# A recurrent block with four heads and a feed-forward part on one Trainium2 core: local attention scores laid out with the keys as rows

## The chip, the core and the metric

The kernel runs on one core of one Trainium2 chip (trn2). A core has TensorE (PE in the profile; its weight loads are PEld), VectorE (DVE), ScalarE (ACT), GpSimd (POOL) and SyncE (SP, which here only issues DMAs). The metric is the device time of one execution in microseconds (us). Everything is float32, and each float32 matmul of the program shows as two passes in the trace.

## The reference

The input is x, 8 sequences of 1024 tokens of 512 numbers. One layer is computed:

```
xn = layernorm(x)
s  = concat(local(xn), sparse(xn), memory(xn), prediction(xn)) @ warboss_w + warboss_b
g  = silu(relu(xn @ w1 + b1) @ w2 + b2)          # 512 -> 2048 -> 512
out = x + s * g

local :  softmax(q k^T / sqrt(128)) v            # all 1024 keys
sparse:  the same with its own weights, but only the 102 largest scores of a row count
memory:  attention over a bank of 64 rows, then a linear layer
prediction: three linear layers with a gelu
```

The change lies in `local`. For each of the 8 sequences it makes a 1024 x 1024 matrix of scores, takes each query's softmax over the keys, and multiplies by v. Its weights are scaled so that the scores are large, so the softmax needs each query's maximum taken off first.

## The kernel before, in words

A sequence b has 8 tiles of 128 tokens (i), 4 pairs of tiles (p, 256 tokens, T) and 2 groups (g, 512 tokens). Tokens are normalized and turned so that features lie on the partitions (`xnT`, `turn_tokens`, L328). All big products (feed-forward up and down, q, k, the memory and prediction inputs, the output projection) are made block-wise with seven products in place of eight, so sums of weight blocks (`form_chunk`), of tokens (`token_sums`, L535), of hidden values (`hidden_sums`, L627: tile `hs`) and of results (`add_products`: tiles `u` and `m`) are made around the matmuls, nearly all of them on POOL.

**The order of the work** is decided while the program is built. `feed_forward` (L662) is a filler that yields one PE matmul after another. Beside it stand `chains`: generators such as `local`, `sparse`, `memory_head`, which give out a few instructions and then yield either a time or a condition. `run` (L133) always lets the first chain that is due go on and otherwise takes the next matmul of the filler. Time is counted in PE columns (`clock`), and each instruction adds a planned cost to its engine's clock: a transpose 64 columns on PE, a 512-column copy 360 on ACT, a POOL operation 60 + 1.42 for each element, a round of the sparse selection 1552 on DVE. `pool_is_free` (L507) is a condition that holds when POOL's clock is at most 300 columns ahead of PE's. `STEP` (L1068) is the number of columns from the start of one tile to the start of the next. On the chip each engine takes its instructions in exactly the order written, and waits where data are not there yet. PSUM has four buffers (`ring`, L190) for everything but the feed-forward sums.

**Sparse.** `sparse` (L885) makes a tile's scores with queries as rows, and DVE finds the 102nd largest of each row in 13 rounds of MAX8 and MATCH_REPLACE8 (`sparse_select`). The result `es` is scaled, transposed in eight 128x128 blocks (`transpose_probs`, L791: tile `ptp`, copied to `pT`) and multiplied with v (`attend`, L804).

**Local before.** `local` (L820) runs for each tile: two score matmuls of 128 queries by 512 keys (`scores`, tile `sc`), copied by ACT to `el`; DVE takes each row's maximum (`nml`); ACT computes Exp with that as bias and adds up the row's total; DVE inverts the total (`r_l`); ACT scales `el` by it; PE transposes eight blocks into `ptp`, and ACT copies them to `pT` (keys as rows, queries as columns). At the second tile of a pair, `attend` multiplies v with `pT` for 256 queries at once: 8 matmuls of 256 columns, and the copy `head`.

**After local**, `finish_pair` (L976) makes the sums `ho` of the four heads on POOL, the filler makes the output projection (`ph_po`), and gating and the residual follow.

**The start.** `first_tokens` (L1043) normalizes and turns the first sequence's tokens group by group, projects the sparse keys of 512 tokens (`project_k`, L342) and the first queries, and starts `turn_constants` (L272, which turns the biases and the memory bank) and the first token sums.

Of the kernel before, what the change touches and what calls it, by code (L numbers as in the profile page):

```python
# [9 lines left out]
F32 = mybir.dt.float32  # L10
AF = mybir.ActivationFunctionType
# [4 lines left out]
P = 128  # L16
# [4 lines left out]
def kernel(  # L21
# [144 lines left out]
    def transpose(out, in_, ident):  # L166
        pe.transpose(out, in_, ident)
        tick(P // 2)
# [21 lines left out]
    def ring(name, shape):  # L190
        return ps_r.tile(list(shape), F32, tag="r", name=name)
# [96 lines left out]
    qT = {}  # L288
# [3 lines left out]
    def needs(*keys):  # L292
        return lambda: all(k in done for k in keys)
# [45 lines left out]
        if b not in kT:  # L339
            kT[b] = sb.tile([P, 2, S], F32, tag="kT", name=f"kT_{b}")  # L340

    def project_k(b, g, h, w):  # L342

        make_k(b)
        ps = ring(f"pk_{b}_{g}_{h}", (P, 512))
        accumulate(
            ps,
            [w[:, c, ts(h, HD)] for c in range(ND)],
            [xnT[b, g][:, c, :] for c in range(ND)],
            512,  # L350
        )
        copy(kT[b][:, h, ts(g, 512)], ps, 360)
        done.add(("k", b, g, h))

    def project_v(b, q, w):

# [178 lines left out]
    def token_sums(g, name):  # L535

        b, q = divmod(g, NG)
        if g:
            yield needs(*[("xnT", b, 4 * q + j) for j in range(4)])
            yield after("act", 0)  # L540
        t = sb.tile([P, 4, 2, T], F32, tag="t", name=f"t_{name}")
        xs = xnT[b, q]
        b11, b12, b21, b22 = (xs[:, ts(h, 2), ts(j, T)] for h in range(2) for j in range(2))
        on_pool("tensor_sub", t[:, 0], b12, b11)
        on_pool("tensor_sub", t[:, 1], b22, t[:, 0])
        on_pool("tensor_sub", t[:, 2], b22, b12)
        on_pool("tensor_sub", t[:, 3], b21, t[:, 1])
        yield after("pool")
        tokens[g] = (b11, b21, t[:, 1], t[:, 2], t[:, 3], t[:, 0], b22)

    SLOTS = ((1, 4), (6, 5))
# [221 lines left out]
    def scores(b, i, h, s):  # L773

        for c in range(S // 512):
            ps = ring(f"sc_{b}_{i}_{h}_{c}", (P, 512))
            matmul(
                ps, qT[b, i // 2][:, h, ts(i % 2, P)], kT[b][:, h, ts(c, 512)], True, True, 512
            )
            copy(s[:, ts(c, 512)], ps, 360)  # L780

    def normalize(e, total, name):
        r = small.tile([P, 1], F32, tag="r", name=f"r_{name}", bufs=4)
        dve.reciprocal(r, total)
# [19 lines left out]
    def attend(b, p, h):  # L804
        ps = ring(f"pa_{b}_{p}_{h}", (P, T))
        accumulate(
            ps,
            [vv[b][:, k, h, :] for k in range(NT)],
            [probsT[b, p, h][:, k, :] for k in range(NT)],
            T,  # L810
        )
        o = sb.tile([P, T], F32, tag=f"head{h}", name=f"head_{b}_{p}_{h}")
        copy(o, ps, 220)
        heads[b, p, h] = o
        done.add(("head", b, p, h))

    def before_pair(b, p):
        return [] if (b, p) == (0, 0) else [("joined", *divmod(b * NP + p - 1, NP))]

    def local(b, i):  # L820
        yield needs(("q", b, i // 2), *[("k", b, g, LOCAL) for g in range(NG)])
        yield after("act", 0)
        if (b, i) != (0, 0):
            yield needs(("pT", *divmod(b * NT + i - 1, NT), LOCAL))
        e = sb.tile([P, S], F32, tag="el", name=f"el_{b}_{i}")
        scores(b, i, LOCAL, e)
        done.add(("local scores", b, i))
        yield after("act")
        nm = small.tile([P, 1], F32, tag="nm", name=f"nml_{b}_{i}", bufs=4)
        dve.tensor_reduce(nm, e, AX.X, ALU.max, negate=True)  # L830
        on("dve", 740)
        yield after("dve", 100)
        total = small.tile([P, 1], F32, tag="total", name=f"totl_{b}_{i}", bufs=4)
        act.activation(e, e, AF.Exp, bias=nm, accum_out=total)
        on("act", 800)
        yield after("act", 100)
        yield from normalize(e, total, f"l_{b}_{i}")
        yield from transpose_probs(b, i, LOCAL, e)
        if i % 2:
            yield needs(("v", b), *before_pair(b, i // 2))  # L840
            yield after("act")
            attend(b, i // 2, LOCAL)
        done.add(("local", b, i))

    def sparse_scores(b, i):
        s = sb.tile([P, S], F32, tag="s", name=f"s_{b}_{i}", bufs=2)
# [38 lines left out]
    def sparse(b, i):  # L885
        n = b * NT + i
        yield needs(("q", b, i // 2), *[("k", b, g, SPARSE) for g in range(NG)])
        if n > 1:
            yield needs(("chosen", n - 2))
        yield max(clock["pe"], clock["act"]) + (SLACK if n else 100)  # L890
        s = sparse_scores(b, i)
        done.add(("sparse scores", n))
        yield after("act")
        o = {}
        rounds.append(sparse_select(b, i, s, o))
        yield lambda: "nm" in o
        if n:
            yield needs(("pT", *divmod(n - 1, NT), SPARSE))
        e = sb.tile([P, S], F32, tag="es", name=f"es_{b}_{i}")
        act.activation(e, s, AF.Exp, bias=o["nm"])  # L900
        on("act", 700)
        o["e"] = e
        yield lambda: "total" in o
        done.add(("chosen", n))
        yield after("dve", 100)
        yield from normalize(e, o["total"], f"s_{b}_{i}")
        yield from transpose_probs(b, i, SPARSE, e)
        if i % 2:
            yield needs(("v", b), *before_pair(b, i // 2))
            yield after("act")  # L910
            attend(b, i // 2, SPARSE)


    def tmp(name):
# [128 lines left out]
    def first_tokens():  # L1043
        def normalize_tokens(j0, j1):
            for j in range(j0, j1):
                ln_stats(0, j, first_x[j])
            ln_rstd(0, j0, j1)
            return [ln_apply(0, j, first_x[j]) for j in range(j0, j1)]

        due = normalize_tokens(0, 2) + normalize_tokens(2, 4)  # L1050
        for at in range(3):
            load_chunk(at)
        for g in range(NG):
            for j in range(4 * g, 4 * g + 4):
                yield due[j]
                turn_tokens(0, j, first_x[j])
            if g == 0:
                due += normalize_tokens(4, 8)
                form_chunk(0)
            yield after("act", 200)  # L1060
            project_k(0, g, SPARSE, first_k)
            if g == 0:
                project_q(0, 0, first_q)
                start(turn_constants())
                start(token_sums(0, 0), rank=0)
                start(hidden_sums(), rank=-1)

    STEP = int(0.995 * (11775 + NWC * (2 * 7 * T + 2 * 7 * H) // 4))  # L1068
    start(first_tokens())
    start(sparse(0, 0))  # L1070
    run(needs(("sparse scores", 0)))
# [7 lines left out]
    for n in range(B * NT):  # L1079
        b, i = divmod(n, NT)  # L1080
        p = i // 2
        now = begin + n * STEP
        run(lambda: clock["pe"] >= now)
        start(local(b, i))
        if i == 0:
            start(project_values(b), now + 1000)
            if b + 1 < B:
                start(prepare_stats(b + 1), now + (2000 if b else STEP))
        if i == 3 and b + 1 < B:
            start(prepare_tokens(b + 1))  # L1090
        if i % 2:
            def two_heads(b=b, p=p):
                yield needs(("m", b, p), *before_pair(b, p))
                yield after("act")
                t = starts.pop((b, p))
                yield from prediction_head(b, p, t[:, 1])
                yield from memory_head(b, p, t[:, 0])
                start(finish_pair(b, p), rank=2)

            start(two_heads(), now + 1500)  # L1100
        if n + 1 < B * NT:
            start(sparse(*divmod(n + 1, NT)), now + int(0.6 * STEP))
# [35 lines left out]
```

## Time and profile before

| what | us |
|---|---|
| median of three runs | 2895.06 |
| the three runs | 2895.06, 2892.13, 2895.14 |
| the profiled execution | 2892.31 |
| its span, first to last instruction | 2890.3 |
| first matmul starts, last matmul ends | 7.8, 2881.8 |

| engine | busy us | share of the span | instructions |
|---|---|---|---|
| PE | 2848.1 | 99% | 13296 |
| DVE | 2376.7 | 82% | 3202 |
| POOL | 2187.9 | 76% | 2908 |
| ACT | 1672.6 | 58% | 3174 |

Busy time is the time in which at least one instruction of the engine was in flight. Matmuls overlap, so the mean duration of one is longer than the step from one to the next. A row of a group reads: line, engine, operation, out<-in by the program's names, shapes, count, then busy us, mean ns of one, and the idle time of the engine just before these instructions with what ended most of it. Nearly all rows show line 85, a helper that records every operation, so tiles are told apart by their names. The DMA engines are busy between 40 and 70% of each slice, and move 186 GB/s.

### The profile page before, as it was taken

How to read it: one execution, taken by the hardware profiler on the slowest of the kernel's cores; microseconds unless marked ns; L12 is line 12 of the kernel's file. 1: busy time of each engine (PE TensorE's matmuls, PEld its weight loads, DVE VectorE, ACT ScalarE, POOL GpSimd, SP SyncE). 2: the span in 40 equal slices, each digit the busy share in tenths (PEclk: the TensorE clock that was granted, in tenths of full speed). 3: DMA queues.
4: the chain of work that ended last, by engine and by line, in shares of the span. 5: the costliest groups of instructions: out<-in, count | busy, mean ns of one | idle time of the engine just before them, and what ended most of it. 6: DMA issues, size and time to landing. Idle time of an engine off the chain costs nothing. (4 is left out here: it accounts for less than half of the span.)

```text
span 2890.3 us, 38499 instructions
## 1 busy us (share of the span) xinstructions
PE 2848.1 (99%) x13296; PEld 2394.5 (83%) x13296; DVE 2376.7 (82%) x3202; ACT 1672.6 (58%) x3174; POOL 2187.9 (76%) x2908
## 2 busy tenths in 40 slices
PE   8989999999999999999999999999999999999998
PEld 6878888888888888888888888888888888887887
DVE  7999979878698785988769897789967989588696
ACT  3546556665566654656546665556655556465564
POOL 4787867868678696786958879587796887867785
PEclk9999999999999999999999999999999999999999
DMA  5665644655455454454545545455455554544545
GB/s 179 215 243 193 209 160 160 223 179 205 148 178 214 175 201 162 172 213 163 206 165 186 206 177 193 164 204 199 156 196 184 186 203 169 197 146 174 200 168 187
DMA packets 132001, 538.89 MB, mean 186 GB/s; under 512 B 13790, under 2 KB 40432, under 8 KB 131808
## 3 DMA queue, kind: packets, MB, share of 16 engines
q1 hardware_dynamic: 126352, 519.23, 50.7%
q0 software_dynamic: 5456, 17.22, 1.6%
q8 instruction: 105, 1.72, 0.2%
q14 instruction: 88, 0.72, 0.1%
HBM read 500.35 MB, written 36.04 MB: 186 GB/s over the span
## 5 line engine op out<-in xcount | busy, mean ns | idle before, releaser
L85 DVE MAX8 top<-left 128x8 f32<-128x1024 f32 x768 | 943.2, 1228 | 26.7
L85 POOL TENSOR_TENSOR u_up<-u_up 128x256 f32<-128x256 f32 (+1 forms) x640 | 620.8, 976 | 318.7 <-ACT u_up L85 293.9
L85 DVE MATCH_REPLACE8 left<-top,left 128x1024 f32<-128x1024 f32 x704 | 850.6, 1208 | 0.0
L85 PE MATMUL f<-w_down,hs 128*128 128x256 f32 x2048 | 539.0, 380 | 2.1 <-POOL w_down L85 1.7
L85 PE MATMUL ph_up<-t,w_up 128*128 128x256 f32 x2048 | 483.3, 379 | 0.1
L85 PEld LDWEIGHTS f<-w_down,hs 128*128 128x128 f32 x2048 | 383.6, 191 | 61.5 <-issue 9.2
L85 PEld LDWEIGHTS ph_up<-t,w_up 128*128 128x128 f32 x2048 | 383.1, 190 | 60.2 <-issue 12.0
L85 PE MATMUL f<-w_down,h 128*128 128x256 f32 x1536 | 421.7, 380 | 3.4 <-ACT h L85 3.4
L85 ACT COPY u_up<-ph_up 128x512 f32<-128x512 f32 (+1 forms) x512 | 265.5, 531 | 237.8 <-PE ph_up L85 237.2
L85 PE MATMUL ph_up<-xnT,w_up 128*128 128x256 f32 x1536 | 383.1, 380 | 1.4 <-ACT u_up L85 0.9
L85 POOL TENSOR_TENSOR hs<-h 128x128 f32<-128x128 f32 x512 | 241.4, 471 | 171.2 <-PE f L85 135.7
L85 PEld LDWEIGHTS f<-w_down,h 128*128 128x128 f32 x1536 | 288.3, 191 | 50.7 <-issue 9.6
L85 PEld LDWEIGHTS ph_up<-xnT,w_up 128*128 128x128 f32 x1536 | 288.0, 190 | 48.8 <-issue 8.8
L85 PE MATMUL sc<-kT,qT 128*128 128x512 f32 x512 | 240.4, 593 | 0.2 <-ACT el L85 0.2
L85 PE MATMUL pa<-pT,v 128*128 128x256 f32 x1024 | 231.6, 379 | 0.0
L85 ACT ACTIVATE h<-u_up,biasT 128x256 f32<-128x256 f32 x512 | 220.2, 501 | 14.1 <-POOL u_up L85 14.1
L85 DVE TENSOR_REDUCE nml<-el 128x1 f32<-128x1024 f32 x64 | 77.3, 1208 | 181.0 <-ACT el L85 180.8
L85 PEld LDWEIGHTS pa<-pT,v 128*128 128x128 f32 x1024 | 194.4, 190 | 28.1 <-issue 1.0
L85 DVE MAX8 top<-s 128x8 f32<-128x1024 f32 x64 | 78.2, 1223 | 167.7 <-ACT s L85 167.5
L85 ACT COPY pT<-ptp 128x512 f32<-128x512 f32 x256 | 149.5, 588 | 113.7 <-PE ptp L85 113.1
L85 ACT ACT_TABLE_LOAD x139 | 178.3, 1283 | 5.0 <-DVE nms L85 2.0
L85 POOL TENSOR_TENSOR u_po<-u_po 128x256 f32<-128x256 f32 (+1 forms) x155 | 146.4, 951 | 19.8 <-ACT u_po L85 13.4
(151 smaller groups left out, 4574.7 us busy)
## 6 DMA issues: line engine op xcount, KB each, us to landing
w_down<-w_down_dram SPq DMA_DIRECT2D x248, 896.0 KB, 4.7
w_up<-w_up_dram SPq DMA_DIRECT2D x120, 896.0 KB, 4.6
w_po<-w_po_dram SPq DMA_DIRECT2D x62, 896.0 KB, 4.6
xl<-in_L_attn_x_dram SPq DMA_DIRECT2D x64, 256.0 KB, 4.8
xr<-in_L_attn_x_dram SPq DMA_DIRECT2D x64, 256.0 KB, 5.0
out_dram<-xr POOLq DMA_DIRECT2D x62, 256.0 KB, 3.0
xs<-in_L_attn_x_dram SPq DMA_DIRECT2D x56, 256.0 KB, 4.9
w_q<-w_q_dram SPq DMA_DIRECT2D x15, 896.0 KB, 4.6
```

The lines of the kernel that those rows point to most:

```text
L85: r = made(*args, **kwargs)
```

## The change

The scores of `local` are made for a pair of tiles at once with the keys as rows: each of eight key blocks of 128 is the stationary side, the 256 queries are the moving side (tile `sl`). ACT's copies of them go straight into the tile that `attend` reads (`pT`), so these probabilities are not transposed.

- The maximum over keys now lies across partitions and blocks. DVE first reduces the eight blocks, `e.rearrange("p c t -> p t c")`, 2048 elements to 256, read with a stride of 1 KB. `across` then turns the two 128x128 halves on PE (`pma`), DVE reduces them from PSUM to two columns, ACT spreads these over 128 columns each, PE turns them back (`pmb`), and ACT copies: every partition then holds minus the maximum of each query.
- POOL adds that to the scores (four adds of 512), and ACT computes Exp (two of 1024) without bias or total.
- The total is made in the same way: DVE reduces the blocks (for the first four pairs POOL adds them up), and `across` (`pta`, `ptb`) gives its reciprocal on every partition. It is applied after `attend`, as one POOL product on `head`.
- `local` is started for pairs and not for tiles, and it waits for the head of the pair before.
- At the start, the sparse keys are projected for 256 tokens at a time, the constants are turned behind the first pair of tiles, the first token sums are made on DVE instead of POOL, and the first formed chunk of weights comes later.
- `STEP` becomes 25855 columns; it was 25980.

The diff's core:

```diff
-    def project_k(b, g, h, w):
+    def project_k(b, g, h, w, part=0, parts=1):
...
-        copy(kT[b][:, h, ts(g, 512)], ps, 360)
-        done.add(("k", b, g, h))
+        copy(kT[b][:, h, ts(parts * g + part, n)], ps, 360 // parts)
+        if part == parts - 1:
+            done.add(("k", b, g, h))
...
+        on = on_pool if g else on_dve
+        on("tensor_sub", t[:, 0], b12, b11)
...
+    def across(ps_name, part, work, op, negate, name):
+        pt = ring(f"{ps_name}a_{name}", (P, 2, P))
+        for j in range(2):
+            transpose(pt[:, j], part[:, ts(j, P)], ident)
+        of = small.tile([P, 2], F32, tag="of", name=f"of{ps_name}_{name}")
+        dve.tensor_reduce(of, pt, AX.X, op, negate=negate)
+        if not negate:
+            dve.reciprocal(of, of)
+        on("dve", 330)
+        yield after("dve", 200)
+        act.copy(work[:, 2].rearrange("p (j t) -> p j t", j=2), of.unsqueeze(2).to_broadcast([P, 2, P]))
+        on("act", 220)
+        yield after("act", 200)
+        pt = ring(f"{ps_name}b_{name}", (P, 2, P))
+        for j in range(2):
+            transpose(pt[:, j], work[:, 2, ts(j, P)], ident)
+        copy(work[:, 3], pt.rearrange("p j t -> p (j t)"), 220)
...
+    def local(b, p):
...
+        for c in range(0, NT, 2):
+            ps = ring(f"sl_{name}_{c}", (P, 2, T))
+            for u in range(2):
+                matmul(
+                    ps[:, u], kT[b][:, LOCAL, ts(c + u, P)], qT[b, p][:, LOCAL], True, True, T
+                )
+            copy(e[:, c : c + 2], ps, 360)
...
+        dve.tensor_reduce(work[:, 0], e.rearrange("p c t -> p t c"), AX.X, ALU.max)
+        on("dve", 1400)
+        yield after("dve", 200)
+        yield from across("pm", work[:, 0], work, ALU.max, True, name)
+        yield after("act", 200)
+        for c in range(0, NT, 2):
+            yield pool_is_free
+            on_pool(
+                "tensor_add", e[:, c : c + 2], e[:, c : c + 2],
+                work[:, 3].unsqueeze(1).to_broadcast([P, 2, T]),
+            )
+        yield after("pool", 100)
+        for c in range(0, NT, 4):
+            act.activation(e[:, c : c + 4], e[:, c : c + 4], AF.Exp)
+            on("act", 800 - 100 * (c > 0))
+        yield after("act", 100)
+        if n < EARLY:
+            yield pool_is_free
+            on_pool("tensor_add", work, e[:, :4], e[:, 4:])
...
+        else:
+            dve.tensor_reduce(work[:, 0], e.rearrange("p c t -> p t c"), AX.X, ALU.add)
+            on("dve", 1400)
+            yield after("dve", 200)
+        yield from across("pt", work[:, 0], work, ALU.add, False, name)
+        yield needs(("v", b), *before_pair(b, p))
+        yield after("act")
+        o = attend(b, p, LOCAL)
+        yield after("act", 0)
+        yield pool_is_free
+        on_pool("tensor_mul", o, o, work[:, 3])
+        yield after("pool", 0)
+        done.add(("head", b, p, LOCAL))
+
+    EARLY = 4
...
-    STEP = int(0.995 * (11775 + NWC * (2 * 7 * T + 2 * 7 * H) // 4))
+    STEP = int(1.0 * (11519 + NWC * (2 * 7 * T + 2 * 7 * H) // 4))
...
-        start(local(b, i))
+        if i % 2 == 0:
+            start(local(b, p))
```

The loop of `first_tokens` after the change, over pairs of tiles:

```
constants = turn_constants()
for p in range(NT // 2):
    g = p // 2
    for j in range(2 * p, 2 * p + 2):
        yield due[j]
        turn_tokens(0, j, first_x[j])
    if p == 0:
        next(constants)
    yield after("act", 200)
    project_k(0, g, SPARSE, first_k, p % 2, 2)
    if p == 0:
        next(constants, None)
        due += normalize_tokens(4, 8)
    elif p == 1:
        start(token_sums(0, 0), rank=0)
        project_q(0, 0, first_q)
        start(hidden_sums(), rank=-1)
    elif p == 2:
        form_chunk(0)
```

More of the change, by code (lines that the diff above doesn't have):

```diff
@@ L340, in make_k @@
             kT[b] = sb.tile([P, 2, S], F32, tag="kT", name=f"kT_{b}")
-    def project_k(b, g, h, w):
+    def project_k(b, g, h, w, part=0, parts=1):
         make_k(b)
-        ps = ring(f"pk_{b}_{g}_{h}", (P, 512))
+        n = 512 // parts
+        ps = ring(f"pk_{b}_{g}_{h}_{part}", (P, n))
         accumulate(
@@ L348, in project_k @@
             [w[:, c, ts(h, HD)] for c in range(ND)],
-            [xnT[b, g][:, c, :] for c in range(ND)],
-            512,
-        )
-        copy(kT[b][:, h, ts(g, 512)], ps, 360)
-        done.add(("k", b, g, h))
+            [xnT[b, g][:, c, ts(part, n)] for c in range(ND)],
+            n,
+        )
+        copy(kT[b][:, h, ts(parts * g + part, n)], ps, 360 // parts)
+        if part == parts - 1:
+            done.add(("k", b, g, h))
     def project_v(b, q, w):
@@ L543, in token_sums @@
         b11, b12, b21, b22 = (xs[:, ts(h, 2), ts(j, T)] for h in range(2) for j in range(2))
[L544 to L548, printed above, removed]
+        on = on_pool if g else on_dve
+        on("tensor_sub", t[:, 0], b12, b11)
+        on("tensor_sub", t[:, 1], b22, t[:, 0])
+        on("tensor_sub", t[:, 2], b22, b12)
+        on("tensor_sub", t[:, 3], b21, t[:, 1])
+        yield after("pool" if g else "dve")
         tokens[g] = (b11, b21, t[:, 1], t[:, 2], t[:, 3], t[:, 0], b22)
@@ L814, in attend @@
         heads[b, p, h] = o
-        done.add(("head", b, p, h))
+        return o
     def before_pair(b, p):
         return [] if (b, p) == (0, 0) else [("joined", *divmod(b * NP + p - 1, NP))]
-    def local(b, i):
-        yield needs(("q", b, i // 2), *[("k", b, g, LOCAL) for g in range(NG)])
-        yield after("act", 0)
[L823 to L827, printed above, removed]
-        yield after("act")
[L829 to L835, printed above, removed]
-        yield after("act", 100)
[L837 to L843, printed above, removed]
@@ new lines, in local @@
+    def local(b, p):
+        n = b * NP + p
+        name = f"{b}_{p}"
+        yield needs(("q", b, p), *[("k", b, g, LOCAL) for g in range(NG)])
+        yield after("act", 0)
+        if n:
+            yield needs(("head", *divmod(n - 1, NP), LOCAL))
+        e = sb.tile([P, NT, T], F32, tag="pT0", name=f"pT_{name}_0")
+        probsT[b, p, LOCAL] = e
+        for c in range(0, NT, 2):
[5 more added lines that the diff above has]
+            copy(e[:, c : c + 2], ps, 360)
+        for j in range(2):
+            done.add(("local scores", b, 2 * p + j))
+        yield after("act")
+        work = sb.tile([P, 4, T], F32, tag="el", name=f"el_{name}")
+        dve.tensor_reduce(work[:, 0], e.rearrange("p c t -> p t c"), AX.X, ALU.max)
[13 more added lines that the diff above has]
+            on("act", 800 - 100 * (c > 0))
+        yield after("act", 100)
+        if n < EARLY:
+            yield pool_is_free
+            on_pool("tensor_add", work, e[:, :4], e[:, 4:])
+            yield pool_is_free
+            on_pool("tensor_add", work[:, :2], work[:, :2], work[:, 2:])
+            yield pool_is_free
+            on_pool("tensor_add", work[:, 0], work[:, 0], work[:, 1])
+            yield after("pool", 100)
+        else:
[7 more added lines that the diff above has]
+        yield after("act", 0)
+        yield pool_is_free
+        on_pool("tensor_mul", o, o, work[:, 3])
+        yield after("pool", 0)
+        done.add(("head", b, p, LOCAL))
@@ L911, in sparse @@
             attend(b, i // 2, SPARSE)
+            done.add(("head", b, i // 2, SPARSE))
     def tmp(name):
@@ L1052, in first_tokens @@
             load_chunk(at)
-        for g in range(NG):
-            for j in range(4 * g, 4 * g + 4):
+        constants = turn_constants()
+        for p in range(NT // 2):
+            g = p // 2
+            for j in range(2 * p, 2 * p + 2):
                 yield due[j]
                 turn_tokens(0, j, first_x[j])
-            if g == 0:
-                due += normalize_tokens(4, 8)
-                form_chunk(0)
[L1060 to L1066, printed above, removed]
-    STEP = int(0.995 * (11775 + NWC * (2 * 7 * T + 2 * 7 * H) // 4))
+            if p == 0:
+                next(constants)
+            yield after("act", 200)
+            project_k(0, g, SPARSE, first_k, p % 2, 2)
+            if p == 0:
+                next(constants, None)
+                due += normalize_tokens(4, 8)
+            elif p == 1:
+                start(token_sums(0, 0), rank=0)
+                project_q(0, 0, first_q)
+                start(hidden_sums(), rank=-1)
+            elif p == 2:
+                form_chunk(0)
+    STEP = int(1.0 * (11519 + NWC * (2 * 7 * T + 2 * 7 * H) // 4))
     start(first_tokens())
```

## The prediction

> **What bounds the kernel now.** I read the page's busy rows first, then the table of stretches, then PE's rows in order of time, then the groups kept apart by shape. First the page, its busy row and the two rows of slices that matter:
>
> ```profile
> PE 2848.1 (99%) x13296; PEld 2394.5 (83%) x13296; DVE 2376.7 (82%) x3202; ACT 1672.6 (58%) x3174; POOL 2187.9 (76%) x2908
> ...
> PE   8989999999999999999999999999999999999998
> ...
> PEclk9999999999999999999999999999999999999999
> ```
>
> PE is at 90% or more in every slice but the first, the third and the last, at a full clock. Busy PE need not be PE at its pace, so its rows in order of time come next (start, length, work):
>
> ```profile
> 1002.70 0.60 PE L85 MATMUL ptp<-ident,es 128*128 128x128 f32 x4
> 1003.14 0.38 PE L85 MATMUL ptm<-ident,weights 128*128 128x128 f32 x2
> 1003.36 1.88 PE L85 MATMUL sc<-kT,qT 128*128 128x512 f32 x4
> 1005.08 0.60 PE L85 MATMUL ptp<-ident,es 128*128 128x128 f32 x4
> ...
> 1009.40 3.62 PE L85 MATMUL pa<-pT,v 128*128 128x256 f32 x16
> 1012.86 0.38 PE L85 MATMUL f<-w_down,h 128*128 128x256 f32 x1
> ```
>
> The reader is to take starts, not lengths. Four transposes last from 1002.70 to 1003.14, two from 1003.14 to 1003.36: 0.11 us each (0.109 is the commonest step), though the group's mean of one is 274 ns, because they overlap. A pass of 256 columns takes (1012.86-1009.40)/16 = 0.216 us, a score pass of 512 columns 1.72/4 = 0.43 us; every float32 matmul is two passes. With these steps I counted the whole program's PE order: 2830 us. First to last matmul it runs from 7.8 to 2881.8 us, 2874 us. So 44 us are not work at pace; the table of stretches (busy us of each engine, clock) says where:
>
> ```profile
> core 0: us, PE busy (x) PEld busy (x) DVE busy (x) ACT busy (x) POOL busy (x), PEclk, DMA share, GB/s
> ...
> 8.00:20.00 12.00, 9.28 (x26) 5.43 (x26) 10.81 (x28) 2.59 (x7) 5.83 (x7) 1.00 1.09 316
> ...
> 60.00:300.00 240.00, 232.14 (x1066) 192.44 (x1065) 229.62 (x316) 135.23 (x263) 181.04 (x242) 0.99 0.61 211
> 300.00:600.00 300.00, 299.54 (x1413) 253.92 (x1412) 254.67 (x342) 174.09 (x326) 234.11 (x314) 1.00 0.54 191
> ...
> 2882.00:2891.00 9.00, 0.00 (x0) 0.00 (x0) 4.70 (x8) 0.13 (x1) 0.00 (x0) 0.68 0.16 58
> ```
>
> Some 8 us go in the first batch (60 to 300), a few at the start, and 0.5 to 4 in each later 300. PE's work is the time. What is taken off PE is won one for one, as long as DVE and POOL still deliver what PE waits for. The rows that price this:
>
> ```profile
> L85 PE MATMUL ptp<-ident,el 128*128 128x128 f32 x512 | 77.6, 274 | 4.3 <-ACT el L85 2.0 <-ACT u_up L85 1.8 <-ACT u_k L85 0.5
> L85 DVE TENSOR_REDUCE nml<-el 128x1 f32<-128x1024 f32 x64 | 77.3, 1208 | 181.0 <-ACT el L85 180.8
> L85 DVE TENSOR_REDUCE nmm<-weights 128x2 f32<-128x128 f32 x32 | 8.7, 273 | 8.7 <-ACT weights L85 8.7
> L85 POOL TENSOR_TENSOR u_up<-u_up 128x512 f32<-128x512 f32 x256 | 333.4, 1302 | 231.1 <-ACT u_up L85 221.0
> L85 ACT ACTIVATE el<-el,r_l 128x1024 f32<-128x1024 f32 x64 | 73.8, 1153 | 10.4 <-DVE r_l L85 10.3
> L85 ACT COPY pT<-ptp 128x512 f32<-128x512 f32 x256 | 149.5, 588 | 113.7 <-PE ptp L85 113.1
> ```
>
> **PE.** Removed: 512 transposes of `el`. Added: 2 + 2 + 2 + 2 per pair in `across`, 32 pairs, 256; the nearest row is `ptm`, also pairs of transposes, at the same 0.11 us. 256 x 0.109 = 27.9 us less. Scores: 256 passes of 512 columns (0.429) become 512 of 256 (0.216): 0.8 us more; weight loads double, but `pa` loads weights for each 256 columns too and keeps 0.216. The sparse keys in halves change nothing at pace. Sum -27.1 us, all on the path.
>
> **ACT, per pair.** Gone: two scalings (2 x 1.153), four copies of `pT` (4 x 0.588), two accumulator reads (0.19 each), 5.0 us. Added: two broadcast copies and two copies, 128x256; near rows give 0.37 (from PSUM) and 0.41 us (from SBUF), 1.6 us. ACT falls by 32 x 3.5 = 110 us. It is at 58%: worth nothing by itself. New: its Exp waits for POOL's adds, and behind it stand the copies that empty PE's four PSUM buffers.
>
> **POOL, per pair.** Four adds of 512 with a repeated operand (u_up's row has such adds: 1.30) and one product of 256 (0.76): 6.0 us, 191 in all; the first four pairs add sums of about 2.5 + 1.3 + 0.76 us, 18 us; four token differences leave, -5. POOL goes from 2188 to about 2392 of 2865, 83%. What hides it: I walked both POOL queues against PE's order; the hidden sums `hs` are ready on average 28 us ahead of their matmul in both (27.6 after), and past the first 200 us never less than 3.2 us ahead (5.9 before). Without that cover it would cost up to 204 us. The product on `head` waits for ACT's copy, and `hs` queue behind it; the same lead covers that.
>
> **DVE, per pair.** Gone: two maxima (2 x 1.208) and two reciprocals (0.15), 2.7 us. Added: two reductions over 2048 elements, two over 256 from PSUM and one reciprocal. The two reduce rows give 1.04 ns per element: 2.28 us and 0.41 us. Together 5.5 us, or +80 us over the kernel (the first four sums are POOL's): 2377 to 2457 of 2865, 86%.
>
> This is the open price. No row reads DVE's input with a stride, and here every element lies 1 KB from the last. The Trainium skill, "SBUF — State Buffer", section "Door 1: The DMA port swizzle (why `[64,N]` ≈ `[32,N]`)", has a note against it: SBUF serves 16-byte lines, and each access that moves to another line pays. If that means two cycles for each element (my estimate from the page's rule: double the 1.04 ns slope), a reduction takes 4.4 us. "VectorE: DVE Perf Modes", section "Mode 1× (REGULAR) — the baseline", says the opposite for this case: the one-element mode takes any stride, since nothing is packed. The `nml` row, without a stride, already takes 1.04 ns for each element, so there is no double pace that a stride could lose. I take 2.28, keep 4.4 as the upper end; below 2.28 nothing is seen that would go faster.
>
> Does DVE still keep up at 2.28? From the built order I summed DVE's rows from each tile's first MAX8 to the end of its selection, and PE's work from its scores to its `es` transposes. Before, PE's stretch is longer by 10.9 us on average (least 0.7); after, by 17.3 us (least -0.4, then 3.5). For the new transposes, queued in front of everything else on PE, the reduction ends 1 to 6 us ahead of their place in nearly all pairs; the exceptions are the end of the first batch (8.7 us late, where before is 8.5 late too and PE lost its 8 us) and two or three places 1.6 to 3.5 us late. DVE's rounds queue behind the new PSUM reduction, which waits for PE. I charge 3 us for the first batch, where the worst lateness grows from 8.5 to 11.6; bounds 0 and 8.
>
> **Start and tail.** Token differences move from POOL to DVE: four at 0.69 us instead of 1.27, but now ahead of the weight sums. Walking rows: before, PE has done 27.2 us of work when the local keys end at 42.8; after, 28.5 by 43.7. That is -0.4 us; bounds -2 (PE has fewer holes, and its first passes of 512, at 0.86 us until 18 us, go faster) and +2. The store of the first formed chunk and its four sums come later, but the SP order is the same until far past it. At the end PE has 12.5 us of work left behind the last `es` transposes instead of 16.6; DVE's selection is ready for them by 0.4 us (3.0 before). I take 0, upper end +3. DVE's 8.5 us behind PE's last matmul stay.
>
> **Sum.** -27.1 - 0.4 + 3 = -24.5 us on the profiled execution's 2892.3 us (span 2890.3 and 2.0 around it): 2867.8. That execution lies 2.75 us under the median of the runs (2892.1 to 2895.1); I put the median after it 1.2 us higher: 2869.
>
> **Rivals.**
> 1. *Slower: the strided reduction costs two cycles an element.* Place: `across`' first transposes, behind which all of PE's queue stands. At 4.4 us each, my count has the reductions late by a growing amount within a batch, 9 to 11 us at its fourth pair. Eight batches x 9.5 us = 76, less 27: about 2941. Lateness starts near 2.9 us per reduction, break-even is near 3.4 us. For: the skill's line rule, DVE at 86%. Against: the one-element pace, no strided row. 11%.
> 2. *Hand-offs.* Each pair has four new places where PE waits for DVE or ACT. The `es` transposes lost 9.1 us over 128 groups, 0.07 each; if the new 128 lose twice that, 0.15 us, 19 us go: about 2885. 12%.
> 3. *Waits go too.* DVE's selection gains 6 us of room, so some of the 17 us of later gaps close: 2860. 12%.
> That the change doesn't do what it says is excluded: the built order has 256 fewer transposes. The forecast itself: 65%.
>
> **Numbers.** 2857 to 2886 leaves out rival 1 and the edges of rival 2 and of the forecast. A measurement can tell 0.2% from no change, 5.8 us: faster 0.86, same 0.03, slower 0.11.
>
> **What would show it.** Right: 512 `el` transposes gone, 256 new ones at 0.11 us from start to start; the reductions near 2.28 us; PE still 99%; PE idle in 60 to 300 near 11 us; last matmul near 2857 us. Wrong: reductions over 3 us with PE's gaps in front of `pma` and `pta`; PE under 98%; POOL or Exp in front of PSUM copies among PE's releasers.

## The result: slower by 0.4%, and the profile after

The changed kernel takes 2905.9 us (2904.8 to 2907.2, five runs); on the same chip the kernel before took 2895.1 (2892.1 to 2896.3). The ratio is 1.0038, with a 95% interval of 1.0027 to 1.0049: 11 us slower, where the prediction said 26 us faster. The profiled execution has a span of 2903.8 us (before 2890.3) at a mean granted TensorE clock of 0.993 (before 0.997).

From the page of the changed kernel: the busy times, and the slices of PE and of its clock.

```profile
PE 2834.0 (98%) x13312; PEld 2423.2 (83%) x13312; DVE 2550.8 (88%) x3234; ACT 1568.4 (54%) x3045; POOL 2378.3 (82%) x3076
...
PE   8989989999999999999999999999999999999998
...
PEclk9999999999999999999999999999999999999999
```

The slices look as before and are no help here: a slice is 72.6 us long, and what was lost comes in holes of 4.4 us at most. PE is at 98% where 99% was expected. With the prediction's steps from start to start, and no waits, the new order is 2802.9 us of PE work ("at pace"), 27.1 less than before, but from the first matmul's start to the last one's it takes 2886.8 us. So 83.9 us are not work at pace; before they were 43.6. The 27 us came off, and 40 us of new holes and slow stretches were put in. The table of stretches shows where the first part of them lies:

```profile
core 0: us, PE busy (x) PEld busy (x) DVE busy (x) ACT busy (x) POOL busy (x), PEclk, DMA share, GB/s
...
60.00:300.00 240.00, 221.54 (x1017) 186.85 (x1016) 226.04 (x300) 123.64 (x244) 204.10 (x255) 0.96 0.61 209
300.00:600.00 300.00, 287.13 (x1339) 244.27 (x1338) 258.95 (x334) 155.18 (x298) 239.42 (x309) 0.98 0.50 175
```

Idle time of PE is 18.5 us in the first stretch (7.9 before) and 12.9 in the second (0.5 before). The granted clock is down too, 0.96 and 0.98 against 0.99 and 1.00. The groups that answer to the rows that priced the change, by form:

```profile
L85 DVE TENSOR_REDUCE el<-pT 128x256 f32<-128x2048 f32 x60 | 224.2, 3737 | 63.2 <-ACT pT L85 58.3 <-POOL o L85 4.9
L85 POOL TENSOR_TENSOR pT<-pT,el 128x512 f32<-128x512 f32 x128 | 165.8, 1315 | 55.6 <-ACT el L85 55.6
L85 PE MATMUL pta<-ident,el 128*128 128x128 f32 x64 | 13.4, 293 | 19.4 <-DVE el L85 14.2 <-POOL el L85 5.0
L85 DVE TENSOR_REDUCE ofpm<-pma 128x2 f32<-128x256 f32 x32 | 13.1, 411 | 2.2 <-PE pma L85 2.0
L85 PE MATMUL pma<-ident,el 128*128 128x128 f32 x64 | 12.5, 277 | 5.9 <-DVE el L85 5.2 <-ACT pT L85 0.3 <-ACT u_up L85 0.3
```

The first row is the open price of the prediction: 3.74 us for one strided reduction, not 2.28. Its shortest is 3.64 and its longest 3.80, so this is not now and then a wait inside the instruction; it is what one costs. The two PE rows show who pays: PE stands idle 14.2 us ahead of `pta` and 5.2 ahead of `pma` until DVE has written `el`, and 5.0 until POOL has. One such place on DVE in order of time (start, length, work):

```profile
554.53 1.23 DVE L85 MAX8 top<-left 128x8 f32<-128x1024 f32 x1
555.67 3.69 DVE L85 TENSOR_REDUCE el<-pT 128x256 f32<-128x2048 f32 x1
559.27 0.79 DVE L85 TENSOR_SCALAR xl<-xl,mv,rs 128x512 f32<-128x512 f32 x1
```

And PE at that moment; a bracket gives the idle time and what ended it.

```profile
556.90 0.59 PE L85 MATMUL f<-w_down,hs 128*128 128x256 f32 x2
559.41 0.44 PE L85 MATMUL pta<-ident,el 128*128 128x128 f32 x2 [1.92 <-DVE el L85]
...
560.55 0.60 PE L85 MATMUL ptx<-ident,xl 128*128 128x128 f32 x4
560.99 0.60 PE L85 MATMUL f<-w_down,hs 128*128 128x256 f32 x2
```

DVE goes from one instruction to the next and the reduction has nothing in front of it but DVE's own work. It ends at 559.36, PE starts the transposes at 559.41. At 2.28 us it would have ended at 557.95, and the hole would have been about 0.5 us. Four transposes still step by 0.11 us (560.55 to 560.99): PE's prices held.

Not all of the new holes are of this kind. A large one in the first batch is in front of `hs`. PE:

```profile
164.42 0.70 PE L85 MATMUL f<-w_down,h 128*128 128x256 f32 x2 [1.77 <-ACT h L85]
169.18 2.07 PE L85 MATMUL f<-w_down,hs 128*128 128x256 f32 x4 [4.07 <-POOL hs L85]
```

POOL at the same time:

```profile
161.75 2.75 POOL L85 TENSOR_TENSOR u_up<-u_up 128x256 f32<-128x256 f32 x3
164.47 3.71 POOL L85 TENSOR_TENSOR pT<-pT,el 128x512 f32<-128x512 f32 x3
168.14 0.46 POOL L85 TENSOR_TENSOR hs<-h 128x128 f32<-128x128 f32 x1
```

Three of the new additions of the maxima stand in POOL's queue directly ahead of the hidden sums that PE is waiting for. And a hole costs more than its length: in the stretch behind it the granted clock is down (the column after the five engines).

```profile
169.50:173.00 3.50, 3.50 (x10) 2.79 (x10) 3.43 (x5) 0.80 (x2) 3.34 (x9) 0.58 0.23 96
```

The trace's record of the clock has stretches at 0.50, here 3.4 or 6.8 us long. Ahead of the kernel's end there are three before (10.2 us) and eight after (37.4 us); all eight begin inside a PE hole of more than 2 us or within 1 us behind one. 27 us more at half speed are at most 14 us of the 40, since part of them passes inside the holes.

### The profile page after: what moved, and what is told of

Same layout as the page of the kernel before. It is cut to its first block, busy times and chain, and to the rows that moved or that the text cites. A ratio compares the mean times of both kernels' runs of the same rounds, so it can differ in the third digit from the quotient of the medians.

```text
span 2903.8 us, 38721 instructions
## 1 busy us (share of the span) xinstructions
PE 2834.0 (98%) x13312; PEld 2423.2 (83%) x13312; DVE 2550.8 (88%) x3234; ACT 1568.4 (54%) x3045; POOL 2378.3 (82%) x3076
## 5 line engine op out<-in xcount | busy, mean ns | idle before, releaser
L85 POOL TENSOR_TENSOR u_up<-u_up 128x256 f32<-128x256 f32 (+1 forms) x640 | 614.6, 965 | 177.9 <-ACT u_up L85 153.5
L85 DVE TENSOR_REDUCE el<-pT 128x256 f32<-128x2048 f32 x60 | 224.2, 3737 | 63.2 <-ACT pT L85 58.3
L85 POOL TENSOR_TENSOR pT<-pT,el 128x512 f32<-128x512 f32 x128 | 165.8, 1315 | 55.6 <-ACT el L85 55.6
L85 POOL TENSOR_TENSOR m<-m 128x256 f32<-128x256 f32 (+1 forms) x155 | 150.9, 976 | 16.7 <-ACT m L85 12.2
L85 DVE BATCH_NORM_STATS2 st<-xs 128x6 f32<-128x512 f32 x56 | 38.0, 679 | 129.2 <-DMA xs<-in_L_attn_x_dram 129.2
```

What stands on the lines that cost most here:

```text
L85: r = made(*args, **kwargs)
```

## The experiments

My theory after the result: (a) DVE's stride is the larger part, as rival 1 named it but at a price between the two that I had; (b) it hurts because DVE is late, not because DVE is full; (c) the rest is lost in the first batch. Rivals were the hand-offs as such (rival 2), the new start, and POOL. Every ratio is to the kernel before on the same chip.

**The stride alone: `e1_packed`.** Both reductions read the same 2048 numbers in packed order, so they reduce wrong groups.

```diff
-        dve.tensor_reduce(work[:, 0], e.rearrange("p c t -> p t c"), AX.X, ALU.max)
+        dve.tensor_reduce(
+                work[:, 0], e.rearrange("p c t -> p (c t)").rearrange("p (a k) -> p a k", k=NT),
+                AX.X, ALU.max,
+            )
```

> The changed kernel with the same order of instructions, in which the two large reductions of a pair read the same 2048 numbers in the order in which they lie (eight neighbours for each output); it so takes maxima and sums over the wrong groups, and nothing else changes. Theory S (the stride made the reductions 3.74 us instead of 2.28, and this alone turned the gain into a loss): they take 2.28 us, PE's idle time falls back to about 45 us, the clock's halved stretches mostly go, and the time is 2865 to 2875 us. Rival H (the hand-offs of the new chain and the fuller POOL hold PE up, whatever the reductions take): reductions 2.28 us, but the time stays above 2890 us.

Measured: 2878.7 us, ratio 0.9946 (0.9933 to 0.9960). The reduction's group:

```profile
L85 DVE TENSOR_REDUCE el<-pT 128x256 f32<-128x2048 f32 x60 | 136.5, 2275 | 69.5 <-ACT pT L85 64.4 <-POOL o L85 4.6 <-POOL t L85 0.3
```

2.275 us, the prediction's price, and 27 us come back. In this order of the work the stride alone decides between slower and faster. But 10 us to the forecast are missing, and they lie ahead of 600 us: PE idles 16.3 us in 60 to 300 and 9.3 in 300 to 600.

**The same work, but planned at its price: `e2_planned`.** The planner was told 1400 columns for a reduction, 2.36 us at PE's 1.69 ns per column (0.43 us for 256). 2250 columns are 3.80 us.

```diff
-        on("dve", 1400)
+        on("dve", 2250)
```

(at both reductions)

> The changed kernel with the planner told the measured price of the large reduction, 2250 columns (3.75 us) instead of 1400; only the order of the work can change. Theory P (the loss is one of placing: the transposes stand 1.4 us too early in PE's queue): PE's waits for DVE el, 24 us in all, fall below 5 us and the time is 2870 to 2885 us. Rival D (DVE simply has too much work in its queue, so that later places only move the waits to the es transposes and the first batch): the time stays at 2895 to 2910 us.

Measured: 2886.1 us, ratio 0.9975 (0.9965 to 0.9985), 1 us above the range of theory P, with the reduction still at 3.75 us. PE's rows:

```profile
L85 PE MATMUL pta<-ident,el 128*128 128x128 f32 x64 | 12.3, 274 | 3.2 <-POOL el L85 1.7 <-DVE el L85 1.4
L85 PE MATMUL pma<-ident,el 128*128 128x128 f32 x64 | 12.2, 273 | 0.3 <-DVE el L85 0.3
```

20 of the 27 us come back with as much DVE work as before: the time that PE waits for DVE ahead of `pta` and `pma` falls from 19.4 to 1.7 us. (The 24 us of the expectation were these 19.4 and 5.0 for POOL.) That bears (b) out: DVE at 89% of the span is not the bound; most of the loss came with an order built on the wrong price. The stretch from 60 to 600 us is not mended by it: PE idles 31.2 us there, as in the changed kernel (31.3).

**Another way to reduce: `e3_fold`.** Three packed two-input operations (1024, 512, 256 results) in place of one strided reduction.

```diff
+    def fold(work, e, op):
+        dve.tensor_tensor(work, e[:, :4], e[:, 4:], op)
+        dve.tensor_tensor(work[:, :2], work[:, :2], work[:, 2:], op)
+        dve.tensor_tensor(work[:, 0], work[:, 0], work[:, 1], op)
...
-        dve.tensor_reduce(work[:, 0], e.rearrange("p c t -> p t c"), AX.X, ALU.max)
+        fold(work, e, ALU.max)
```

> The changed kernel with the large reduction made of three two-input operations of 1024, 512 and 256 elements, none with a stride. At the pace of the two-input rows (690 ns for 512) they take 1.2 + 0.7 + 0.4 = 2.3 us if POOL does not hold them up, and the time is near that of the packed reduction, 2865 to 2880 us. If they have to wait for POOL's operations, as two-input DVE rows of this trace do (0.94 us for 256 elements against 0.42 alone), they take 3.5 to 5 us and the time is 2890 to 2915 us, the same as or worse than the strided reduction.

Measured: 2905.8 us, ratio 1.0043 (1.0028 to 1.0058), in time the second case of the expectation. From the first operation's start to the third's end a fold takes 3.3 us on average, but between 2.4 and 5.3, and 16 of the 60 take longer than the strided 3.74. Where POOL is idle the three take 1.22, 0.69 and 0.42 us; where POOL is at work they take longer. One such fold on DVE, and POOL at the same time:

```profile
721.20 2.13 DVE L85 TENSOR_TENSOR el<-pT 128x1024 f32<-128x1024 f32 x1
723.37 1.42 DVE L85 TENSOR_TENSOR el<-el 128x512 f32<-128x512 f32 x2
```

```profile
720.98 1.27 POOL L85 TENSOR_TENSOR u_po<-u_po 128x512 f32<-128x512 f32 x1
722.21 1.43 POOL L85 TENSOR_TENSOR hs<-h 128x128 f32<-128x128 f32 x1
```

DVE's first operation takes 2.13 us instead of 1.22, since about 1 us of POOL's running sum is still to come when it starts; then POOL's `hs` takes 1.43 us instead of 0.46. For the operation with 512 results this is regular: the 16 that start with POOL free, or 0.12 us before it is, take 0.69 us, and each of the other 44 takes longer by what is left of POOL's running instruction, less 0.14 us. The strided reduction, which has one input, does not show it: 3.64 to 3.80 us, though POOL works beside 59 of the 60. So 0.4 us saved on average came with a scatter that makes some folds later than before, and PE still waits 20.1 us for DVE ahead of `pta` and `pma`.

**The start alone: `e4_start`.** The kernel before with nothing but the new start (the keys for two tiles at a time, the constants turned in the first gap, the first token sums on DVE, the first formed chunk later); the local attention is that of before.

```diff
-        for g in range(NG):
-            for j in range(4 * g, 4 * g + 4):
+        constants = turn_constants()
+        for p in range(NT // 2):
+            g = p // 2
+            for j in range(2 * p, 2 * p + 2):
...
-            project_k(0, g, SPARSE, first_k)
+            project_k(0, g, SPARSE, first_k, p % 2, 2)
```

> The kernel before with the start of the changed one alone (sparse keys for two tiles at a time, constants in the first gap, first token sums on DVE, first chunk formed later). By the prediction this is worth 0.4 us, bounds -2 to +2: 2893 to 2897 us. If the first batch's extra 10 us of idle PE in the changed kernel come from the start, with weight sums pushed behind the token sums on DVE, this kernel shows them: 2900 us or more.

Measured: 2886.1 us, ratio 0.9973 (0.9962 to 0.9984): 7 us faster, where the prediction had 0.4. PE's work is only some 1.4 us ahead at 60 us. The rest comes later: 36.3 us not at pace, against 43.6, and between 600 and 2700 us PE idles 8.6 us instead of 14.3. That this is due to the other order in which the later work then falls is inferred.

**The early sums on POOL: `e5_early0` and `e7_packed_early0`.** The first four pairs' sums go to DVE like all others; the one on top of `e2_planned`, the other on top of `e1_packed` (so with its wrong groups).

```diff
-    EARLY = 4
+    EARLY = 0
```

> The changed kernel with the large reduction planned at 2250 columns (2886.1 us so far) and, besides, no sums on POOL for the first four pairs: DVE makes all 64 reductions. Theory F (the losses left in the first 600 us come from POOL, whose early sums of 4.4 us a pair stand in front of the transposes pta and of hs): PE's idle time between 60 and 600 us falls from 31 us to some 15 and the time is 2870 to 2877 us. Rival G (DVE has no room there, with weight sums and statistics in its queue, and POOL's sums were a relief): 2886 to 2900 us.

> The changed kernel with packed reductions (2278.7 plus 600, that is 2878.7 us so far; maxima and sums over the wrong groups) and no early sums on POOL. Theory F: the first 600 us lose 10 us less and it reaches the forecast, 2866 to 2871 us. Rival G: 2876 us or more.

Measured: 2886.05 us, ratio 0.9975 (0.9967 to 0.9983), and 2881.0 us, ratio 0.9955 (0.9940 to 0.9971): no gain in either. The early sums do not hold the missing 10 us, though PE is seen waiting 4.2 us for one of them after the change. Without them there are other holes in their place: in `e5_early0` PE waits 16.0 us for DVE ahead of `pta` (1.4 in `e2_planned`).

**The old start with the new attention: `e6_old_start`.** `e2_planned` with the start of before, `e4_start`'s diff undone.

> The changed kernel with the large reduction planned at 2250 columns, and the start of the kernel before put back (keys for four tiles at a time, constants later, token sums on POOL). If the start's 7 us, seen in the kernel before, is a gain of its own, this one is about 7 us slower than with the new start: 2890 to 2896 us. If those 7 us were a matter of how the later order happened to fall, the difference has no fixed sign: 2880 to 2890 us.

Measured: 2881.1 us, ratio 0.9959 (0.9947 to 0.9971): 5 us faster than with the new start. The start that gave 7 us to the old attention takes 5 from the new one. So it has no fixed price of its own; what it changes, as far as is seen, is which operations meet in the queues. The table of stretches shows where:

```profile
60.00:300.00 240.00, 220.07 (x999) 185.95 (x998) 220.76 (x297) 119.72 (x233) 199.50 (x253) 0.96 0.59 199
300.00:600.00 300.00, 298.62 (x1419) 256.79 (x1418) 271.46 (x347) 167.40 (x320) 254.25 (x331) 1.00 0.54 190
```

PE's idle time in 300 to 600 is down to 1.4 us (12.3 in `e2_planned`), that in 60 to 300 is not (19.9), and between 600 and 2700 it is up again (14.1 against 5.2). The 5 us are the balance.

**What a stride costs by itself: `e8_stride`.** No kernel of this computation: six DVE reductions each over eight elements that lie 1, 2, 3, 4, 8, 32 or 256 places of 4 bytes apart (`ra` to `rg`), with nothing else running; 2048 elements each, for three places 2040.

```
for b in (1, 2, 3, 4, 8, 32, 256):
...
            if b == 3:
                v = e[:, : 3 * 8 * 85].rearrange("p (a k b) -> p a b k", k=8, b=3)
...
            else:
                v = e.rearrange("p (a k b) -> p a b k", k=8, b=b)
```

> A kernel of nothing but DVE reductions of 2048 numbers to 256, six each with the eight numbers of a group 1, 2, 3, 4, 8, 32 and 256 places apart (4 bytes to 1 KB); it computes nothing of the reference. If the price of a stride begins where each number lies in another 16-byte line, places 1 to 3 take 2.28 us, 4 and more take 3.7 us, all alike. If it grows with the distance, 4 and 8 are cheaper than 256. If 3.74 us in the changed kernel came from other engines working beside DVE, all take 2.28 us here.

Measured, its groups:

```profile
L62 DVE TENSOR_REDUCE re<-e 128x256 f32<-128x2048 f32 x6 | 22.8, 3807 | 0.0
L62 DVE TENSOR_REDUCE rd<-e 128x256 f32<-128x2048 f32 x6 | 22.6, 3770 | 0.0
L62 DVE TENSOR_REDUCE rg<-e 128x256 f32<-128x2048 f32 x6 | 21.5, 3590 | 0.1
...
L62 DVE TENSOR_REDUCE rc<-e 128x255 f32<-128x2040 f32 x6 | 17.1, 2856 | 0.0
L62 DVE TENSOR_REDUCE ra<-e 128x256 f32<-128x2048 f32 x6 | 13.7, 2277 | 2.5 <-DMA e<-in_L_attn_x_dram 2.5
L62 DVE TENSOR_REDUCE rb<-e 128x256 f32<-128x2048 f32 x6 | 13.7, 2275 | 0.0
```

Two places apart cost nothing (1.11 ns per element, as for one), three 1.40 ns, four 1.84, and beyond that it stays: eight 1.86, 32 and 256 some 1.75. So the price does not grow with the distance; it is full from 16 bytes on. The Trainium skill's note in "SBUF — State Buffer", section "Door 1: The DMA port swizzle (why `[64,N]` ≈ `[32,N]`)", agrees if all of it is read: an access that moves to a new 16-byte line pays, but two hits on a line are enough for full speed. Two places apart give two hits on each line, four and more only one. The prediction took the first half alone, by which two places would have cost something too. The note has no figure; here a line for each element costs 0.64 to 0.75 ns more per element. Within the kernel the reduction takes 3.74 us and alone 3.59: nearly all of it is intrinsic.

**POOL's additions in the first batch: `e9_no_adds`.** `e1_packed` without the additions of the maxima for the first four pairs (the planner is charged as if they were there).

```diff
             yield pool_is_free
+            if n < NP:
+                on("pool", 60 + int(1.42 * 2 * T))
+                continue
             on_pool(
...
-            act.activation(e[:, c : c + 4], e[:, c : c + 4], AF.Exp)
+            act.activation(e[:, c : c + 4], e[:, c : c + 4], AF.Exp, scale=0.01 if n < NP else 1.0)
```

> The kernel e1_packed, with POOL's four additions of the maxima left out for the four pairs of the first batch (their scores go to the exponential as they are, scaled by 0.01 there, so that the first batch's local attention is another function; the reductions read packed numbers in all batches as in e1_packed). The planner is still charged for the additions, so the order of everything else is meant to stay. The question is the 10 us that e1_packed (2878.7 us) still lies above the forecast, all of it lost before 600 us. Theory G: in the first batch POOL's additions (some 1.3 us each, three or four of them in a row) stand in front of hs and of the sums of w_down for which TensorE waits; without them TensorE is busy about 229 us or more of the stretch 60 to 300 us (223.7 in e1_packed, 232.1 before) and the time is about 2870 us (2867 to 2873). Rival H: not POOL's load but the longer chain of hand-offs of a pair and the order that follows from it: TensorE stays at 222 to 225 us there and the time at 2876 to 2880 us.

Measured: 2868.9 us, ratio 0.9915 (0.9901 to 0.9928). This is the time of theory G, 10 us under `e1_packed`, for 16 additions of 1.3 us. The edit takes out a wait too: the Exp of these four pairs no longer stands behind POOL and the maxima, so the 10 us belong to the additions together with that wait. The hole in front of `hs` has closed; PE at that place:

```profile
161.22 0.70 PE L85 MATMUL f<-w_down,h 128*128 128x256 f32 x2 [1.67 <-ACT h L85]
162.32 1.70 PE L85 MATMUL f<-w_down,hs 128*128 128x256 f32 x4 [0.40 <-POOL hs L85]
```

The table of stretches says less than theory G wanted:

```profile
60.00:300.00 240.00, 226.72 (x1048) 192.72 (x1047) 223.43 (x306) 125.02 (x247) 192.55 (x251) 0.97 0.64 217
300.00:600.00 300.00, 294.92 (x1398) 252.59 (x1397) 263.41 (x350) 161.12 (x311) 245.04 (x321) 1.00 0.52 180
```

226.7 us busy in 60 to 300, not 229 or more (223.7 in `e1_packed`), and 294.9 in 300 to 600 (290.7). Together 7.2 us less idle. The 4.4 us in front of `u_up`, at 283 in the changed kernel, stay (4.6 us at 278), and 3.7 us in front of `es` at 180 are new.

**Everything at once: `e10_packed_old_start`.** `e6_old_start` with the packed reductions of `e1_packed` (its diff, so wrong groups).

> The kernel e6_old_start (the start of before, the planner charged 2250 columns for a reduction) with the packed reductions of e1_packed (wrong groups of eight in maxima and sums, so another function): the change without its new start, without its stride and with its price planned. If what the stride costs and what start and plan cost add up, the time is about 2872 us (2869 to 2876), near the 2869 us of the forecast. If the plan already hides the stride, the time stays at 2879 to 2882 us, as e6_old_start.

Measured: 2879.6 us, ratio 0.9951 (0.9938 to 0.9963), against 0.9959 for `e6_old_start`. With the old start and the price in the plan, what the stride costs is lost in the noise (1.5 us between the medians, and the intervals of the ratios overlap), where it was 27 us in the changed kernel. The plan still charges 2250 columns for the packed reduction here. The two gains do not add up.

**A shorter step: `e11_short_step`.** `e6_old_start` with `STEP` down from 25855 to 25599 columns, 0.43 us for each of 64 tiles. (The change had already taken 256 columns out of the sum in `STEP`, 11775 to 11519, and put 130 back with the factor, 0.995 to 1.0; this run takes 256 out a second time, so `STEP` was not as "unshortened" as the expectation has it.)

```diff
-    STEP = int(1.0 * (11519 + NWC * (2 * 7 * T + 2 * 7 * H) // 4))
+    STEP = int(1.0 * (11519 - 256 + NWC * (2 * 7 * T + 2 * 7 * H) // 4))
```

> The kernel e6_old_start (2881.1 us) with the planner's step from tile to tile shortened by 256 columns (11519 becomes 11263 in STEP), the TensorE columns of which the change rid each tile. If the unshortened step makes work start later than TensorE could take it, the shorter one gains: 2874 to 2878 us. If the step only shifts the order, the time stays within 4 us of 2881, to either side.

Measured: 2924.7 us, ratio 1.0102 (1.0087 to 1.0118), outside both expectations. PE is down to 588.5 of 600 us in 1200 to 1800 and 583.3 in 1800 to 2400 (594.0 and 594.3 in `e6_old_start`). The holes are in front of `ptm`, `ph_po`, `ptp` and `pta`, which wait for DVE, POOL and ACT. So with tiles started 1% sooner PE arrives there before the other engines are through. A longer step was not tried.

**The additions on DVE: `e12_dve_adds`.** `e6_old_start` with the first batch's 16 additions on DVE.

```diff
-            on_pool(
+            (on_dve if n < NP else on_pool)(
...
-        yield after("pool", 100)
+        yield after("dve" if n < NP else "pool", 100)
```

> The kernel e6_old_start (2881.1 us; real reductions, the start of before, 2250 columns planned for a reduction) with the sixteen additions of the maxima of the first batch's four pairs given to VectorE instead of GpSimd (planner charged 340 columns each, as for its other two-input work). By the runs before, these additions cost some 10 us where they stand in front of hs and of the sums of w_down on GpSimd. If it is their place on GpSimd that costs, and VectorE has room: 2870 to 2876 us. If VectorE, busy 221 of 240 us there in e6_old_start, has no room for sixteen operations of 0.75 us and the weight sums behind them come later: 2880 to 2888 us.

Measured: 2880.5 us, ratio 0.9950 (0.9937 to 0.9964): the second case, though not for its reason.

```profile
60.00:300.00 240.00, 227.71 (x1036) 191.71 (x1035) 225.25 (x309) 123.50 (x245) 194.58 (x250) 0.96 0.60 206
300.00:600.00 300.00, 290.12 (x1357) 247.58 (x1356) 271.45 (x338) 161.52 (x308) 237.80 (x311) 0.98 0.51 180
```

Against the rows of `e6_old_start`, PE gains 7.6 us in 60 to 300 and gives back 8.5 in 300 to 600, where it waits 2.2 and 2.8 us for POOL's `ho` at 346 and 349, and 1.6 us for ACT's `h` at 550. The holes moved. In the first of these stretches, where Exp waits for the additions as before and only their engine is another, this supports POOL's load as the cause there; over the whole kernel it wins nothing. Of the kernels that compute the whole function, this one and `e6_old_start` are the fastest, 0.4 to 0.5% faster than before and 0.8 to 0.9% faster than the change.

## Why the prediction was wrong, step by step

- **PE, -27.1 us: right.** The counted order went from 2830.0 to 2802.9 us at pace, and transposes still step by 0.11 us.
- **ACT, -110 us and off the path: right** (-104). That its Exp waits for POOL's additions, with PSUM copies behind it, is not where PE lost: Exp waited 3.0 us in all. The one long PE wait for an ACT copy, 4.4 us at 283 for `u_up`, comes from ACT waiting 7.5 us for POOL's `o`, and it is there without the additions too (`e9_no_adds`).
- **POOL, +204 us and hidden: right in size** (+190, an addition 1.31 us), **wrong in "hidden".** The mean lead of `hs` is the forecast's (27.6 us in the trace after) and was no help. I excepted the first 200 us from the least lead and charged them nothing for POOL. There, three additions stand straight ahead of `hs`; `e9_no_adds` puts 10 us on the first batch's 16 additions and the wait for them.
- **DVE, +80 us at 2.28 us per reduction: this is the step that failed first.** A strided reduction takes 3.74 us, 1.64 times the packed one, so DVE grew by 174 us (with the packed order 91, near the 80). Of the two rules weighed, I sided with the Trainium skill's "VectorE: DVE Perf Modes", section "Mode 1× (REGULAR) — the baseline". It says that strides work in that mode and gives no price for them; I took that as free. For two places `e8_stride` bears it out, from three on it does not. The line note of "SBUF — State Buffer", which spoke against the change, was right. My estimate from it, 4.4, was 0.66 us too high. `e1_packed` puts the size of this step at 27 us.
- **Rival 1 (11%) is what happened, in its place, at a smaller size.** Its place, `across`' first transposes, held. Its break-even of 3.4 us stays untested, since `e3_fold`'s 3.3 us are an average over 2.4 to 5.3. What was wrong was its chance. A price bounded by 2.28 and 4.4, with a break-even of 3.4 in between and no strided row in the profile, does not allow 11% for the upper half.
- **DVE's lateness was no property of its load.** I counted it on the built order and took that order as given. The planner was charged 2.36 us. With 3.80 (`e2_planned`), the same DVE work costs the kernel 20 us less, and with the old start too the stride's cost is not clear of the noise (`e10_packed_old_start`).
- **First batch, +3 us (0 to 8): too small.** Idle time in 60 to 600 grew from 8.3 to 31.3 us in the changed kernel, and to 25.6 even with the packed reductions. I had looked at DVE's lateness alone there.
- **Start, -0.4 us (-2 to +2): wrong.** -7 us on the old attention, +5 on the new one with its planned price. It was summed as work, and most of its effect comes later than the start itself.
- **Tail, 0: right behind the last matmul** (9.0 us, before 8.6). Ahead of it, from 2700 us on, PE idles 4.1 us in the changed kernel, 0.8 in `e1_packed` and not at all before: the stride again, not a term of its own.
- **Rival 2**, 0.15 us at each of 128 groups: not so. The waits ahead of `pta` and `pma` are few and long (17 on DVE and POOL, 24.4 us). **Rival 3**: in the changed kernel the later holes did not close (15.4 us idle between 600 and 2700, before 14.3). They do close once DVE is on time: 7.7 us in `e1_packed`, 5.2 in `e2_planned`.

With the stride and the first batch's additions both out, the time is 2868.9 us, and 45.8 us are not at pace (before 43.6). That it is the forecast's 2869 is in part luck. PE still idles 18.4 us between 60 and 600 (8.3 before, to which the forecast added 3), and only 7.9 between 600 and 2700 (14.3 before, of which the forecast took nothing off): two errors of 6 to 7 us that cancel. The stretch behind 600, before and in `e9_no_adds`:

```profile
600.00:2700.00 2100.00, 2085.70 (x9789) 1760.11 (x9788) 1705.48 (x2271) 1237.10 (x2352) 1612.77 (x2126) 1.00 0.51 183
600.00:2700.00 2100.00, 2092.11 (x9924) 1799.98 (x9923) 1800.43 (x2324) 1174.89 (x2281) 1772.53 (x2286) 1.00 0.54 186
```

Nor do the two terms add up in any order: the two removed in another order (`e10_packed_old_start`, `e12_dve_adds`) give no such gain. What remains open is why, in the kernels with the old start and the planned price, 57 to 60 us stay not at pace. The repairs tried there moved the holes or made more of them.

## What to carry to other kernels

When a price is open and the break-even lies inside its bounds, the chance of the bad side is not small, whatever rule one prefers; and here one reduction measured with the layout at hand would have settled it. Where a planner orders the work, a wrong price in the plan can make up most of what a dear operation costs (here 20 of 27 us), so measure first and tell the planner, before taking the operation out. For a new load on a helper engine, read its lead at the tightest stretch (here the first batch, with the forming of the weights), since the mean over the kernel hides the place that pays.

## What the hardware showed that was not expected

- A VectorE reduction of 2048 float32 numbers takes 2.28 us when the eight members of a group are 4 or 8 bytes apart, 2.86 at 12 bytes (2040 numbers), 3.77 at 16 bytes and 3.59 at 1 KB (`e8_stride`).
- A two-input VectorE operation that starts while GpSimd runs a two-input one takes longer by nearly all that is left of it: in `e3_fold` 0.69 us for 512 results grows to as much as 1.65. The reductions with one input do not. Splitting a reduction into two-input steps puts it into that queue three times.
- In the changed kernel each of the eight holes of over 2 us in PE's work (behind the first matmul) goes with 3.4 or 6.8 us at a granted clock of 0.50. It is no sharp line: in the kernel before, a hole of 2.23 us at 648 has none and one of 1.99 at 176 has. Behind the 4.07 us hole that ends at 169.18 the passes of 256 columns step by 0.43 us instead of 0.216 until the clock comes back at 172.4, so the hole cost about 1.6 us (half of 3.2) more than its length.
